# Layer 0's q and k projections as three one-pass products of exact 12-bit parts, with v's projection moved ahead of and between their blocks

## The chip, the cores and the metric

The kernel runs on one core of one Trainium2 chip. A core has TensorE (PE, matrix products, with its weight loads shown apart as PEld), VectorE (DVE), ScalarE (ACT), GpSimd (POOL) and SyncE (SP), which here only issues transfers. The metric is the device time of one execution in microseconds (us); lower is better.

## The reference, cut to what matters

Eight images of 384 channels by 32x32 positions go through two attention layers. The change lies in layer 0 alone:

```python
qkv = (tokens @ qkv_w + qkv_b).reshape(b, n, 3, NUM_HEADS, HEAD_DIM)   # n = 1024, 8 heads of 48
q, k, v = ...
attn = jnp.einsum('bhnd,bhmd->bhnm', q * scale, k) + bias[None]
attn = jax.nn.softmax(attn, axis=-1)
out = jnp.einsum('bhnm,bhmd->bhnd', attn, v)
...
x = x + out @ proj_w + proj_b          # tokens are the group-normalised x
```

All of it is float32. Layer 1 follows: a second attention (6 heads of 64) and a feed-forward part, which takes images 0 to 4 alone.

## The kernel before

The kernel works through layer 0 image by image and then through layer 1 image by image. The order of the instructions on each engine is the order in which the program is written (a manual schedule): each engine takes its instructions in that order, and semaphores alone decide when one may start. SP's order of transfers is the program's order too, so a transfer that waits holds back those behind it.

**Small works by steps.** `later.after(n, work)` puts a piece of work off until `later.step()` has been called n more times; a step is called after each unit of the attention loop and after each block of a projection.

**One image of layer 0.** The image lies in SBUF as `xn`, three tiles of 128 channels by 1024 positions, and is normalised in place. Each q or k projection of a pair of heads is one block (a pair is numbered 0 to 2, `s` is 0 for q and 1 for k, six blocks in all; the fourth pair's channels ride in spare rows of the other three and are copied out by DMA). A block (line 475) is 6 float32 products of 128x128 weights with 128x512 positions, summed over three channel tiles `k` into one PSUM buffer of 128x1024. DVE (line 485, q) or ACT (line 489, k) adds the bias and writes `qk[pair][:, s]`. v's projection (line 503) is four blocks of 6 products of 384 columns, each taken by two DVE adds (line 508).

**The attention loop** runs over 32 units (pair, half of the queries, quarter of the keys). In a unit PE makes the scores of two heads (`s`, line 529), then weighs with the exponentials of the unit two earlier (`o`, line 560; `LAG = 2`). DVE adds the position bias to the scores (line 540, two instructions), and ACT takes the exponential (line 544). Every fourth unit ends an `o`: ACT copies one half (line 568), DVE adds the other (line 571), and after the second half of a pair `divide` sends the sums through DRAM, inverts them on POOL (line 589), spreads them (line 597), multiplies on POOL (line 601), and for the fourth pair issues six copies (line 611). Two units' weighing is left when the loop ends.

**Between two images** the order on PE is: q and k of the next image (six blocks), the two weighings left over, v of the next image (four blocks), the next image's units.

**Buffers.** All PSUM is one pool of four buffers of 128x1024 (`mm2`). Exponentials, and most temporary tiles of 128x1024, come from one pool of nine (`etile`, tag `e`). `qkp` has four q/k tiles. The weights of q, k and v lie in one tile of the tag `w`, of which there is one.

**One-pass products elsewhere.** In layer 1's feed-forward part (lines 1578 and 1629) the operands have the type fp32r, with the activation split into a high and a low part; a matmul on such operands is one instruction record in the trace, while each float32 matmul is two.

## Time and profile before

| | us |
|---|---|
| median of 3 runs | 3038.91 (3038.33 to 3039.49) |
| span of the profiled execution | 3031.8 |
| PE busy in that span | 3010.9 |
| DVE busy | 1777.3 |
| ACT busy | 1401.8 |
| POOL busy | 470.2 |
| one transition between two images of layer 0, image 1 to 2 (364.64 to 415.02) | 50.4 |

The profile is one execution; its span begins with the first instruction and ends with the last, and the measured time lies 7.1 us above it. Busy PE time is the time in which some matmul record is open; records are pipelined and overlap, so that the step from the start of one record to the start of the next, not a record's duration, tells what it costs in a row of many. Rows of groups give line, engine, operation, tiles, shapes and count, then busy us and mean ns of one, then the idle time of the engine before them and what ended it.

### The profile page before, as it was taken

Reading aid. Unit: us, or ns where it says so; the run is one execution under the profiler, and the core shown is the slowest. Engines: PE = TensorE matmul, PEld = TensorE weight load, DVE = VectorE, ACT = ScalarE, POOL = GpSimd, SP = SyncE. Lnnn points to the kernel's source line nnn. Section 1 sums busy time; section 2 is a strip of 40 time slices with the busy share of each in tenths; the row PEclk is TensorE's granted clock in tenths of the full one; section 3 lists DMA queues with packets and bytes.
Section 4 is the critical chain, followed back from the end, with each engine's and each line's share of the span. In section 5 each row is a group of like instructions: output and inputs, shape, how many; then the busy total and the mean of one; then the engine's idle time right before and its main releaser. Section 6 shows DMA issues by size and latency. Waiting matters only on the chain.

```text
span 3031.8 us, 45645 instructions
## 1 busy us (share of the span) xinstructions
PE 3010.9 (99%) x18902; PEld 1622.9 (54%) x18902; DVE 1777.3 (59%) x1765; ACT 1401.8 (46%) x1757; POOL 470.2 (16%) x314
## 2 busy tenths in 40 slices
PE   8999999999999999999999999999999999999999
PEld 3555546455554645555545655655655655645453
DVE  3746637374654727364565765765765755755646
ACT  2633526253452615254463553553653543653534
POOL 2111102121110202102202202202202202211110
PEclk9999999999999999999999999999999999999999
DMA  7512020210202021121401101101101101102011
GB/s 199 146 26 83 19 83 17 72 37 19 83 19 83 23 72 30 26 99 51 116 27 37 50 16 37 50 23 30 50 23 30 50 23 30 50 16 72 16 51 38
DMA packets 102425, 153.47 MB, mean 51 GB/s; under 512 B 59648, under 2 KB 63216, under 8 KB 101184
## 3 DMA queue, kind: packets, MB, share of 16 engines
q1 hardware_dynamic: 98944, 148.63, 17.0%
q8 instruction: 152, 2.49, 0.3%
q10 hardware_dynamic: 3264, 1.82, 0.2%
q14 instruction: 65, 0.53, 0.1%
HBM read 112.29 MB, written 29.07 MB: 47 GB/s over the span
## 4 chain that ended last, share of the span: by engine, by line
PE 93%; DVE 2%; DMA 2%; SPq 1%; ACT 1%; POOL 0%; issue 0%; DVEq 0%; ACTq 0%; POOLq 0%
PE s L529 15%; PE o L560 15%; PE s L1337 11%; PE o L1386 11%; PE pq L475 8%; PE y2p L1629 6%; PE pq L1193 5%; PE pp L624 4%; PE pv L1274 4%; PE y1p L1578 4%; PE pp L1483 4%; PE pv L503 4%; SPq L399 1%; PE sum L1413 1%; PE hs L1222 1%; DVE lun L1530 1%
## 5 line engine op out<-in xcount | busy, mean ns | idle before, releaser
L544 ACT ACTIVATE e<-e 128x1024 f32<-128x1024 f32 x512 | 535.0, 1057 | 441.1 <-DVE e L540 419.9
L540 DVE TENSOR_TENSOR e<-s,grow 128x1024 f32<-128x1024 f32 x512 | 601.1, 1218 | 186.3 <-PE s L529 186.3
L529 PE MATMUL s<-qk 48*64 48x512 f32 x4096 | 607.8, 591 | 2.8 <-DVE e L540 2.7
L560 PE MATMUL o<-e,v 64*64 64x512 f32 x4096 | 603.8, 589 | 0.0
L1348 ACT ACTIVATE e<-s,kc 128x512 f32<-128x512 f32 x768 | 463.9, 694 | 170.6 <-PE s L1337 160.0
L1337 PE MATMUL s<-qk,qk 64*64 64x512 f32 x3072 | 418.3, 592 | 0.2
L1386 PE MATMUL o<-e,v 64*64 64x512 f32 x3072 | 414.8, 590 | 0.0
L529 PEld LDWEIGHTS s<-qk 48*64 48x64 f32 x4096 | 242.2, 132 | 222.1 <-issue 74.9
L560 PEld LDWEIGHTS o<-e,v 64*64 64x64 f32 x4096 | 266.7, 133 | 171.0 <-issue 63.0
L1363 DVE TENSOR_TENSOR t<-t,e 128x1024 f32<-128x1024 f32 x192 | 230.9, 1221 | 53.9 <-ACT e L1348 53.9
L1337 PEld LDWEIGHTS s<-qk,qk 64*64 64x64 f32 x3072 | 153.5, 132 | 189.9 <-issue 110.3
L1193 PE MATMUL pq<-bx,wqkv 128*128 128x512 f32 x576 | 254.1, 596 | 0.7 <-ACT tra L1165 0.7
L475 PE MATMUL pq<-xn,w 128*128 128x512 f32 x576 | 251.8, 598 | 0.0
L1386 PEld LDWEIGHTS o<-e,v 64*64 64x64 f32 x3072 | 157.6, 133 | 171.1 <-issue 143.8
L589 POOL TENSOR_TENSOR inv<-sums,over 128x16 f32<-128x16 f32 x32 | 92.8, 2900 | 956.9 <-DMA sums<-sd 785.4
L475 PEld LDWEIGHTS pq<-xn,w 128*128 128x128 f32 x576 | 109.4, 191 | 142.4 <-issue 139.9
L1193 PEld LDWEIGHTS pq<-bx,wqkv 128*128 128x128 f32 x576 | 107.8, 190 | 143.5 <-issue 139.7
L1360 DVE TENSOR_TENSOR t<-e,e 128x1024 f32<-128x1024 f32 x96 | 114.1, 1224 | 83.0 <-ACT e L1348 83.0
L1565 DVE TENSOR_REDUCE parts<-y 128x1 f32<-128x1024 f32 x75 | 90.1, 1217 | 93.7 <-ACT y L1562 93.2
L1243 POOL TENSOR_TENSOR hc<-hc,rsqrt 128x32 f32<-128x32 f32 x24 | 139.0, 5793 | 2.0
L1209 ACT ACTIVATE qsq<-pq 128x1024 f32<-128x1024 f32 x48 | 49.2, 1025 | 190.1 <-DVE qk L1203 101.9
L485 DVE TENSOR_SCALAR qk<-pq,bqk 128x1024 f32<-128x1024 f32 x24 | 30.8, 1283 | 178.3 <-PE pq L475 178.3
(166 smaller groups left out, 3034.3 us busy)
## 6 DMA issues: line engine op xcount, KB each, us to landing
rb<-rd SPq DMA_DIRECT2D x110, 256.0 KB
xn<-in_x_dram SPq DMA_DIRECT2D x24, 512.0 KB
res<-in_x_dram SPq DMA_DIRECT2D x24, 512.0 KB
x<-res SPq DMA_DIRECT2D x24, 512.0 KB
bx<-x SPq DMA_DIRECT2D x8, 1536.0 KB
rq<-hi SPq DMA_DIRECT2D x48, 256.0 KB
out_dram<-bx SPq DMA_DIRECT2D x23, 512.0 KB
wide<-table SPq DMA_DIRECT2D x80, 114.2 KB
```

Of the source, the lines that this page charges most:

```text
L475: nc.tensor.matmul(pq[:, h], wqk[:, k, s, 2 * pair : 2 * pair + 2, :].rearrange("p h d -> p (h d)"), xn[:, k, ts(h, HALF)], start=(k == 0) ...
L529: nc.tensor.matmul(s[j][ts(c, QP), i], qk[pair][rows, 1, ts(4 * m2 + 2 * i + c, QP)], qk[pair][rows, 0, ts(h, HALF)], start=True, stop=True,)
L540: nc.vector.tensor_add(e.rearrange("p (i q) -> p i q", i=2), s[j], bass.AP(near.tensor, near.offset, [near.ap[0], [-QROWS * IW, 2], [1, HA ...
L544: nc.scalar.activation(e, e, AF.Exp)
L560: nc.tensor.matmul(po[ts(j, S0), r], v[keys, 2 * m2 + i, 2 * pair + j, :], es[j][keys, ts(i, HALF)], start=(m2 == 0 and i == 0), stop=(m2 ...
L1193: nc.tensor.matmul(pq[:, h], wqkv[:, k, s * C + pair * P : s * C + (pair + 1) * P], xt[:, k, ts(h, HALF)], start=(k == 0), stop=(k == KC - 1),
L1243: nc.gpsimd.tensor_tensor(c, c, rsqrt.to_broadcast(list(c.shape)), ALU.pow)
L1337: nc.tensor.matmul(s[j][ts(c, QP), i], qk[pair, 1][rows, ts(4 * m2 + 2 * i + c, QP)], qk[pair, 0][rows, ts(h, HALF)], start=True, stop=True,)
L1348: nc.scalar.activation(e[:, ts(i, HALF)], s[j][:, i], AF.Exp, scale=kc[:, pair, j, m : m + 1])
L1363: nc.vector.tensor_add(total[j], total[j], e)
L1386: nc.tensor.matmul(po[ts(j, D1), r], v[keys, 2 * m2 + i, at : at + D1], es[j][keys, ts(i, HALF)], start=(m2 == 0 and i == 0), stop=(m2 == ...
L1629: nc.tensor.matmul(py[m][:, h], w2[:, k, ts(m, P)], supply.parts[k][i][:, ts(h, HALF)], start=(k == 0 and i == 0), stop=(k == FC - 1 and i ...
```

## The change

q and k of images 1 to 7 are no longer float32 products. The activation and the weights are each cut into parts that hold 12 significant bits: `high` (the low 12 bits of the float's pattern masked off), `low` (the rest), and `high - 4096 low`. A block is then three products of these parts, each over three channel tiles and two halves: high by high and low by 4096 low into one PSUM buffer (`pg`), the two differences into another (`pm`). `pg (1 + 1/4096) - pm / 4096` is the product. So a block has 18 one-pass matmuls in place of 6 float32 ones, two PSUM buffers in place of one, and is taken by ACT (from `pm`, with the bias) and then DVE (from `pg`).

The weights are cut once, during image 0: three pieces of work, put 18, 21 and 24 steps behind, which fall into units 17, 20 and 23. Each has four DVE instructions and one ACT copy on 128x768, takes five `e` tiles and writes three parts to DRAM. From unit 26 of image 0 the tag `w` holds the parts of three blocks at a time; after each of the first three blocks of a transition, that block's place is loaded with the block three further on, and the next transition begins with the three blocks that are there.

The activation is cut per image: three masks on DVE behind units 26, 27 and 28, into q/k tiles that are free then; three ACT copies, three DVE subtractions and three DVE differences at the transition. These nine parts fill the nine `e` tiles.

The order on PE in a transition becomes: first block of v, one weighing, the other weighing, second block of v, three blocks of q/k, third and fourth block of v, three blocks of q/k.

`wv` has a tile of its own, and `bq` holds q's bias times its scale (one small POOL instruction). Image 0's own projections, and layer 1, are as they were.

```diff
-        both = shared.weights("w0")
-        wqk = both[:, 0 : KC * 2 * C].rearrange(
-            "p (k s h d) -> p k s h d", k=KC, s=2, d=S0
-        )
-        wv = both[:, KC * 2 * C :].rearrange("p (k c) -> p k c", k=KC)
+        plain = shared.weights("w0")[:, 0 : KC * 2 * C]
+        wqk = plain.rearrange("p (k s h d) -> p k s h d", k=KC, s=2, d=S0)
+        wv = const.tile([P, KC, C], F32, tag="wv", name="wv")
+        bq = const.tile([P, NF0], F32, tag="bq", name="bq")
...
-        def project_v(b, xn):
-            for m2 in range(MT // 2):
+        blocks = [(pair, s) for pair in range(NF0) for s in range(2)]
+        BB = len(blocks) // 2
+        cut = dram.tile([len(blocks), P, 3, KC, P], F32, tag="cut", name="cut", bufs=1)
+        def masked(out, of):
+            nc.vector.tensor_single_scalar(
+                out.bitcast(INT), of.bitcast(INT), MASK, op=ALU.bitwise_and
+            )
+        def cut_weights(k):
+            w = plain[:, ts(k, 2 * C)]
+            high, low = etile(f"ch{k}")[:, 0 : 2 * C], etile(f"cl{k}")[:, 0 : 2 * C]
+            parts = [etile(f"c{i}_{k}", dtype=F32R)[:, 0 : 2 * C] for i in range(3)]
+            masked(high, w)
+            nc.scalar.copy(parts[0], high)
+            nc.vector.tensor_sub(low, w, high)
+            nc.vector.tensor_scalar_mul(parts[1], low, CUT)
+            nc.vector.scalar_tensor_tensor(parts[2], low, -CUT, high, ALU.mult, ALU.add)
+            for i, part in enumerate(parts):
+                nc.sync.dma_start(
+                    cut[:, :, i, k].rearrange("n p c -> p n c"),
+                    part.bitcast(F32).rearrange("p (n c) -> p n c", c=P),
+                )
+        class Cut:
+            def __init__(self):
+                t = shared.pool.tile([P, KC * 3 * C], F32R, tag="w", name="wc")
+                self.w = t.rearrange("p (n i k c) -> p n i k c", n=BB, i=3, k=KC)
+            def load(self, n):
+                pair, s = blocks[n]
+                nc.sync.dma_start(
+                    self.w[:, n % BB].rearrange("p i k c -> p (i k c)").bitcast(F32),
+                    cut[s * NF0 + pair].rearrange("p i k c -> p (i k c)"),
+                )
+        class Ahead:
...
+            def high(self, k):
+                return self.tile(k // 2)[:, k % 2]
+            def mask(self, k):
+                masked(self.high(k), self.xn[:, k])
+            def highs(self):
+                self.parts = [[], [], []]
+                for k in range(KC):
+                    t = etile(f"xh{self.b}_{k}", dtype=F32R)
+                    nc.scalar.copy(t, self.high(k))
+                    self.parts[0].append(t)
+            def low(self, k):
+                t = etile(f"xl{self.b}_{k}", dtype=F32R)
+                nc.vector.tensor_sub(t, self.xn[:, k], self.high(k))
+                self.parts[1].append(t)
+            def mixed(self, k):
+                t = etile(f"xd{self.b}_{k}", dtype=F32R)
+                nc.vector.scalar_tensor_tensor(
+                    t, self.parts[1][k].bitcast(F32), -CUT, self.high(k), ALU.mult, ALU.add
+                )
+                self.parts[2].append(t)
+            def project(self, weights, n):
+                pair, s = blocks[n]
+                t = self.tile(pair)[:, s]
...
+                ps = mm2("pg" + name), mm2("pm" + name)
+                for i in range(3):
+                    for k in range(KC):
+                        for h in range(NH):
+                            nc.tensor.matmul(
+                                ps[i // 2][:, h], weights.w[:, n % BB, i, k],
+                                self.parts[i][k][:, ts(h, HALF)],
+                                start=(k == 0 and i != 1), stop=(k == KC - 1 and i != 0),
+                            )
+                by = D0**-0.5 if s == 0 else 1.0
+                nc.scalar.activation(
+                    t, flat2(ps[1]), AF.Identity, scale=-by / CUT,
+                    bias=bq[:, pair : pair + 1] if s == 0 else bqk[:, s, pair : pair + 1],
+                )
+                nc.vector.scalar_tensor_tensor(
+                    t, flat2(ps[0]), by * (1.0 + 1.0 / CUT), t, ALU.mult, ALU.add
+                )
+                last = self.tile(NF0)
+                for j in range(2):
+                    nc.sync.dma_start(
+                        last[j * S0 + pair * FR : j * S0 + (pair + 1) * FR, s],
+                        t[j * S0 + D0 : (j + 1) * S0],
+                    )
+                later.step()
+        def project_v(b, xn, some=range(MT // 2)):
+            for m2 in some:
...
+        nc.gpsimd.tensor_scalar(bq, bqk[:, 0], D0**-0.5, 1.0, ALU.mult, ALU.mult)
+        for k in range(KC):
+            later.after(18 + 3 * k, lambda k=k: cut_weights(k))
...
                 later.step()
-            if b + 1 < B:
-                qk = project_qk(b + 1, xn)
-            for done in held:
-                finish = weigh(b, *done)
+                if i == 26 and b == 0:
+                    weights_qk = Cut()
+                    for n in range(BB):
+                        weights_qk.load(n)
+                if b + 1 < B and i >= 26 and i < 26 + KC:
+                    if i == 26:
+                        ahead = Ahead(b + 1, xn)
+                    ahead.mask(i - 26)
+            def weigh_held():
+                finish = weigh(b, *held.pop(0))
                 if finish is not None:
                     finish()
-            if b + 1 < B:
-                project_v(b + 1, xn)
...
+            order = [n % len(blocks) for n in range(b % 2 * BB, b % 2 * BB + len(blocks))]
+            def project(some):
+                for n in some:
+                    ahead.project(weights_qk, n)
+                    if n in order[:BB]:
+                        weights_qk.load((n + BB) % len(blocks))
+            ahead.highs()
+            for k in range(2):
+                ahead.low(k)
+            project_v(b + 1, xn, [0])
+            weigh_held()
+            ahead.low(2)
+            weigh_held()
+            ahead.mixed(0)
+            project_v(b + 1, xn, [1])
+            for k in range(1, KC):
+                ahead.mixed(k)
+            project(order[:BB])
+            project_v(b + 1, xn, [2, 3])
+            project(order[BB:])
+            qk = ahead.qk
```

More of the change, by code (lines that the diff above doesn't have):

```diff
@@ L61 @@
 LAG = 2
+CUT = 4096.0
+MASK = -4096
+INT = mybir.dt.int32
 class _Later:
@@ L205, in _layer0, with etile @@
         rsqrt = shared.rsqrt
-        def etile(name, shape=(P, N)):
-            return ep.tile(list(shape), F32, tag="e", name=name)
+        def etile(name, shape=(P, N), dtype=F32):
+            return ep.tile(list(shape), dtype, tag="e", name=name)
         def flat2(t):
@@ new lines, in _layer0, with __init__, tile @@
+        class Ahead:
+            def __init__(self, b, xn):
+                self.b, self.xn = b, xn
+                self.qk = {}
+            def tile(self, pair):
+                if pair not in self.qk:
+                    self.qk[pair] = qkp.tile([P, 2, N], F32, tag="qk", name=f"qk{self.b}_{pair}")
+                return self.qk[pair]
+            def high(self, k):
[21 more added lines that the diff above has]
+                t = self.tile(pair)[:, s]
+                name = f"{self.b}_{pair}_{s}"
+                ps = mm2("pg" + name), mm2("pm" + name)
[22 more added lines that the diff above has]
+                later.step()
@@ L707, in _layer0 @@
                 later.step()
-            if b + 1 < B:
-                qk = project_qk(b + 1, xn)
-            for done in held:
-                finish = weigh(b, *done)
+                if i == 26 and b == 0:
[8 more added lines that the diff above has]
+                finish = weigh(b, *held.pop(0))
                 if finish is not None:
                     finish()
-            if b + 1 < B:
-                project_v(b + 1, xn)
+            if b + 1 == B:
+                while held:
+                    weigh_held()
+                break
+            order = [n % len(blocks) for n in range(b % 2 * BB, b % 2 * BB + len(blocks))]
[10 more added lines that the diff above has]
+            ahead.low(2)
+            weigh_held()
+            ahead.mixed(0)
[6 more added lines that the diff above has]
+            qk = ahead.qk
         for m in range(KC):
```

## The prediction

> **What bounds the kernel now.** I read the page's totals first, then the chain of waits in order of time around a transition between two images of layer 0, then the timelines of PE and DVE.

> ```profile
> span 3031.8 us, 45645 instructions
> PE 3010.9 (99%) x18902; PEld 1622.9 (54%) x18902; DVE 1777.3 (59%) x1765; ACT 1401.8 (46%) x1757; POOL 470.2 (16%) x314
> PE 93%; DVE 2%; DMA 2%; SPq 1%; ACT 1%; POOL 0%; issue 0%; DVEq 0%; ACTq 0%; POOLq 0%
> ```

> PE is busy throughout and is 93% of the chain that ended last, so what PE no longer does comes off the time, unless a new wait takes its place. The chain at the first transition:

> ```profile
> 188.54 1.72 PE o L560 x15
> 190.26 31.10 PE pq L475 x72
> 221.35 3.60 PE o L560 x32
> 224.95 15.68 PE pv L503 x48
> 240.63 5.85 PE s L529 x45
> ```

> It is all PE: 50.4 us from the first q/k matmul to the first scores (50.37 and 50.38 at the first two transitions). The six blocks take 31.1 us; 72 records at 0.4288 us each would be 30.87, and the remaining 0.2 us is the switch to the next kind. What a one-pass matmul costs is in this trace too, in layer 1's feed-forward part:

> ```profile
> 1641.30 0.62 PE L1578 MATMUL y1p<-lun,w 128*128 128x512 f32 x2
> 1641.75 0.63 PE L1578 MATMUL y1p<-un,w 128*128 128x512 f32 x2
> 1642.22 0.62 PE L1578 MATMUL y1p<-lun,w 128*128 128x512 f32 x2
> 1642.68 0.62 PE L1578 MATMUL y1p<-un,w 128*128 128x512 f32 x2
> ```

> Two matmuls start every 0.463 us, so one costs 0.2316 us (the durations overlap). DVE's prices come from the groups:

> ```profile
> L540 DVE TENSOR_TENSOR e<-s,grow 128x1024 f32<-128x1024 f32 x512 | 601.1, 1218 | 186.3 <-PE s L529 186.3
> L1618 DVE SCALAR_TENSOR_TENSOR ly<-y,hy 128x1024 fp32r<-128x1024 f32 x60 | 74.1, 1235 | 14.9 <-PE y2p L1629 11.3
> L1617 DVE TENSOR_SCALAR hy<-y 128x1024 fp32r<-128x1024 f32 x60 | 41.5, 691 | 10.3 <-ACT y L1609 9.9
> L640 DVE SCALAR_TENSOR_TENSOR res<-pp,bp,res 128x1024 f32<-128x1024 f32 x24 | 30.8, 1284 | 88.8 <-PE pp L624 88.8
> L489 ACT ACTIVATE qk<-pq,bqk 128x1024 f32<-128x1024 f32 x24 | 26.7, 1114 | 210.0 <-PE pq L475 210.0
> ```

> The last view shows what DVE work in the attention loop costs, in image 0:

> ```profile
> 127.63 0.69 DVE L571 TENSOR_TENSOR oT<-o,oT 128x512 f32<-128x512 f32 x1 [1.33 <-ACT oT L568]
> 128.57 0.65 DVE L411 COPY grow<-oT 128x480 f32<-128x480 f32 x1 [0.24 <-DMA oT<-table]
> ...
> 129.14 1.28 DVE L426 BATCH_NORM_STATS2 gst<-xn 128x6 f32<-128x512 f32 x2
> 130.33 2.34 DVE L540 TENSOR_TENSOR e<-s,grow 128x1024 f32<-128x1024 f32 x2
> ...
> 131.59 1.51 PE L529 MATMUL s<-qk 48*64 48x512 f32 x11 [1.81 <-DVE e L540]
> ```

> A unit takes 3.44 us; DVE's two adds take 2.36 and leave a gap of 1.08 us. Here three works stood in one gap, the adds came about 3.0 us late (130.33 in place of about 127.3), and PE lost about 2.5 us (its scores of the unit after next start at 134.67, where 3.44 us a unit gives 132.2). So work of up to 1.08 us behind a unit is free, some 0.55 us more is absorbed, and the rest stops PE.

> [...] a float32 matmul is two records of 0.4288 us[...]; a fp32r one is a single record. [...] the feed-forward shows 231.6 ns, and I take that, keeping 214.4 as the lower end. [...] the trace's two spreads of 256 KB (line 597 issued at 354.00, POOL released at 358.67) took 4.7 us.

> **PE, per transition.** Removed: 72 records x 0.4288 = 30.87 us. Added: 6 blocks x 18 x 0.2316 = 25.01 us. v (48 x 0.3225 = 15.48) and two weighings (3.44) stay. Switches between kinds of matmul cost 0.1 to 0.23 us each (PE's gap before and after line 1222 near 1646.5 is 0.1 and 0.14); there are four before, 0.68 us together, and seven after, about 1.15. Before: 50.47 (50.4 seen). After: 25.01 + 15.48 + 3.44 + 1.15 = 45.08. Gain 5.4 us.

> **What must be ready for the first block.** Let T be the end of the weighing of unit 29. v's first block ends at T + 4.0, the weighings at 5.9 and 7.65, v's second block at 11.7; the first q/k block starts at 11.8 and needs its last `mixed` part 16 matmuls later, at 15.5. DVE in its order: adds of unit 31 until 0.8; two `low`, 1.22 each, until 3.25; v's adds until 5.2; third `low`, which waits for an `e` tile from the first weighing (5.9), until 7.35; line 571, which waits for ACT's copy (8.45), until 9.2; first `mixed` 1.235 until 10.45; v's adds when block two ends, until 12.9; two `mixed` until 15.4. That is just in time: I charge 0.1 us. ACT's three copies (1.05 each, line 1526's price) are over at 5.05, behind the exponentials.

> **Taking the blocks.** ACT 1.11 and DVE 1.28, in series, 2.5 us after a block of 4.17; with four PSUM buffers the next but one is free in time. At the end nothing hides it: DVE is busy with the last block until T' + 2.65 (T' is PE's end), while before, v's last adds were over sooner and line 540 began at 2.2 us after v's end (417.00 against 414.8). DVE sets the pace of the first three units (six adds in a row, 6.88 us), so PE gets this delay: 0.48 us.

> **Weights.** A block's place is loaded (590 KB, about 5 us by the 4.7 above) once PE is done with it, but on SP behind that block's copies, which wait for DVE, and for the third block also behind the six copies of line 611, which wait for POOL and take 4.4 us to issue. With sums out at 9.3, POOL's inverse at 12.4 to 15.3, spread at 19.4, product by 26 and the copies at 27.6 to 32, the third load is issued at 32 and lands at 37.6; its block starts at 40.6. Margin 3 us, cost 0. Without this cover each us late costs 7 us in all.

> **Masks.** One-source, 0.69 us in a gap of 1.08, no line 571 in units 26 to 28: free. No bitwise operation is in the trace; at the two-source price, 1.22, it would be 0.14 over and absorbed.

> So a transition gains 5.4 - 0.1 - 0.48 = 4.8 us, seven of them 33.6 us.

> **Image 0, cutting the weights.** Four DVE instructions on 768 columns: the one-source ones 0.56 each and the two-source ones 0.96 [...], 3.04 and about 3.1 with their waits on each other. Unit 17 also has line 571 and a batch-norm step: the gap is full, 3.3 us late, PE loses 2.8. Units 20 and 23: 3.1 - 1.08 - 0.55 = 1.5 each. The parts hold three `e` tiles until they have landed in DRAM, 393 KB each[...], and those of unit 17 are issued behind `divide`'s wait on POOL (6.8 us after line 571, as 142.82 to 149.63 shows); unit 20's exponentials need these tiles some 10 to 13 us after it. About 1 us more, 0 to 8 at the bounds. Sum 7 us, from 4 to 15. The first three loads have 17 us of units and 11.8 more: hidden.

> **Sum.** 33.6 - 7 = 26.6 us. Span 3031.8 - 26.6 = 3005.2; the runs stand 7.1 us above the span, so the median goes from 3038.9 to 3012.3.

> **Rivals.**
> - *One-pass matmuls reach 214.4 ns*, since a weight is used twice in a row: 756 x 17.2 ns = 13 us more, 2999.3. Against it: the feed-forward uses each four times in a row and shows 231.6. Chance 0.07.
> - *The cut costs more*: the tiles held by DRAM writes, whose 512-byte runs I have no measurement of, bring image 0 to 16 us: 3021.3. For it: SP's queue is blocked just there. Chance 0.10.
> - *Late parts or loads in every transition, moderately*: DVE's chain has no margin at its end, one instruction later is 1.2 us; the third load 1 us past its margin the like. 2 us each, 14 us: 3026.3. Chance 0.11.
> - *Slower: the third load sets the transition.* Place: the sixth block of each transition, PE waiting for a DMA. Price: 7 us for each us beyond the 3 us of margin; with 33.6 - 7 = 26.6 us of gain, slower from 3.8 us of wait on, that is a landing 6.8 us later than worked out. With 6 us of wait, 42 us: 3054.3. For it: SP takes its transfers in order and waits on POOL and DVE ahead of this load. Against it: every step of that chain has its time in the trace. Chance 0.07.

> **How the numbers follow.** My case 0.65, 3012.3; its own range 3006 to 3018 (4.2 to 5.4 us a transition, 5 to 12 us in image 0). The range of 3002 to 3027 takes in the dear cut, the moderate lateness and half of the cheap case. A measurement of this kernel tells 0.2%, 6.1 us, from no change. Faster by more: 0.65 + 0.07 + 0.10 and nearly all of the 0.11, 0.90; within: 0.03; slower 0.07.

> **What would show it.** PE's step in the q/k blocks 0.23 us and a block 4.2; transitions of 45 us; the first line 540 of an image 2.6 us after PE's last block; no PE wait on a DMA in the transitions; PE waits on DVE of 1.5 to 3 us in units 18 to 24 of image 0 alone. Wrong it would be by a step near 0.29 us (18 of them are 5.15 us, the old block), or by waits at the sixth block.

## The result and the profile after

The changed kernel takes 3005.78 us (median of 4 runs, 3004.06 to 3011.10) against 3039.20 us for the kernel before beside it: a ratio of 0.9898, 95% interval 0.9884 to 0.9912. That is 33.4 us less. The profiled execution of after is the run of 3006.06 us.

The head of its page, as for before (busy us, share of the span, instructions):

```profile
span 3004.1 us, 46389 instructions
PE 2974.7 (99%) x19154; PEld 1640.6 (55%) x19154; DVE 1871.5 (62%) x1861; ACT 1447.9 (48%) x1802; POOL 469.4 (16%) x315
```

PE is 36 us less busy than before, and the span is 27.7 us shorter. The difference went into idle time of PE, and most of that lies in image 0, as will be seen. Line numbers of after that recur below: 590 is the q/k block, 596 and 600 its taking by ACT and DVE, 577 the making of a `mixed` part (the difference high - 4096 low), 616 v's projection, 642 the scores and 653 the adds (529 and 540 before), 508 the mask and 520 to 522 the other DVE instructions of the weights' cut, 460 the normalisation and 714 the multiplication on POOL.

First the chain of waits of after in the transition from image 0 to 1 (start us, us, engine, tile, line):

```profile
199.76 4.07 PE pv L616 x12
...
211.49 2.79 PE pg L590 x12
214.28 1.40 PE pm L590 x6
...
243.01 1.42 PE pm L590 x6
244.46 1.12 ACT qk L596
245.60 1.23 DVE qk L600
246.83 2.27 DVE e L653 x2
```

PE has no gap from 199.76 to 244.46: 44.70 us, where before had 50.37. Six matmuls take 1.40 us, that is 0.2333 us each, and a block 4.20. The new thing is the end: ACT and DVE take the last block before DVE can add the bias to the first scores, so the first line 653 begins 2.28 us after PE's last block, where before had 1.93 us (240.63 to 242.56). So a transition gains 5.67 - 0.35 = 5.3 us. The period of an image says the same: 169.14 us after, 174.45 before, 5.31 us for each of seven.

Image 0 pays. This is DVE behind unit 20, in the timeline of after (start us, us, engine, line, operation, tiles, shapes, count, idle time before and who ended it):

```profile
155.70 2.35 DVE L653 TENSOR_TENSOR e<-s,grow 128x1024 f32<-128x1024 f32 x2 [1.08 <-PE s L642]
...
159.65 1.35 DVE L521 TENSOR_SCALAR c<-cl 128x768 fp32r<-128x768 f32 x1
...
161.99 2.35 DVE L653 TENSOR_TENSOR e<-s,grow 128x1024 f32<-128x1024 f32 x2
```

and the timeline of POOL:

```profile
158.91 5.11 POOL L460 TENSOR_SCALAR xn<-xn,gsc 128x1024 f32<-128x1024 f32 x3 [7.31 <-DMA gsc<-back]
```

The adds come 6.29 us after the last ones in place of 3.44. And line 521 took 1.35 us, while the same instruction takes 0.56 behind units 17 and 23; POOL's three instructions beside it took 5.11 us in place of the 3.54 that they take with no cut beside them (first experiment on image 0). PE's three new waits on DVE, in the timeline of PE:

```profile
148.64 2.83 PE L642 MATMUL s<-qk 48*64 48x512 f32 x11 [2.55 <-DVE e L653]
163.27 1.51 PE L642 MATMUL s<-qk 48*64 48x512 f32 x11 [2.46 <-DVE e L653]
175.48 1.51 PE L642 MATMUL s<-qk 48*64 48x512 f32 x11 [1.35 <-DVE e L653]
```

The eleven matmuls after the first wait take 2.83 us, after the others 1.51. The windows view says why (window, its length, busy us of PE, PEld, DVE, ACT and POOL, then the granted PE clock, DMA share and GB/s):

```profile
149.00:151.00 2.00, 2.00 (x12) 0.49 (x8) 0.71 (x1) 1.73 (x2) 1.82 (x3) 0.50 0.03 3
...
152.00:154.00 2.00, 2.00 (x24) 0.72 (x20) 1.74 (x2) 0.48 (x1) 0.00 (x0) 1.00 1.01 284
```

After its stall PE ran at half clock, from 148.6 to 152.0 us: 12 matmuls in 2 us, where it made 24 at full clock from 152 to 154 us.

The difference of the two profiled executions adds up, taken from the starts of the line-653 (before: 540) adds in image 0: from the first of unit 17 to that of unit 31 before has 48.12 us (14 units of 3.44) and after 57.25, 9.13 lost. Units 12 to 17 take 19.97 and 21.50, 1.53 lost, although the cut has not begun: there too PE's clock fell to 0.50, from 131.5 to 134.9 us, after a stall that both kernels have (1.81 us). The first add comes 1.02 us sooner, and units 0 to 12 take 0.14 less. So 7 x 5.31 - 9.13 - 1.53 + 1.02 + 0.14 = 27.7 us, the difference of the spans.

### The profile page after: what moved, and what is told of

It reads as the page before. It is cut to its first block, busy times and chain, and to the rows that moved or that the text cites. A ratio compares the mean times of both kernels' runs of the same rounds, so it can differ in the third digit from the quotient of the medians.

```text
span 3004.1 us, 46389 instructions
## 1 busy us (share of the span) xinstructions
PE 2974.7 (99%) x19154; PEld 1640.6 (55%) x19154; DVE 1871.5 (62%) x1861; ACT 1447.9 (48%) x1802; POOL 469.4 (16%) x315
## 4 chain that ended last, share of the span: by engine, by line
PE 90%; DVE 4%; DMA 3%; SPq 2%; ACT 1%; issue 1%; POOL 1%; DVEq 0%; ACTq 0%; POOLq 0%
PE o L673 14%; PE s L642 14%; PE s L1486 11%; PE o L1535 11%; PE y2p L1778 6%; PE pq L1342 5%; PE pp L737 4%; PE pv L1423 4%; PE y1p L1727 4%; PE pp L1632 4%; PE pg L590 4%; PE pv L616 4%; PE pm L590 2%; SPq L403 1%; DVE e L653 1%; PE sum L1562 1%
## 5 line engine op out<-in xcount | busy, mean ns | idle before, releaser
L1535 PE MATMUL o<-e,v 64*64 64x512 f32 x3072 | 414.8, 590 | 0.0
L642 PEld LDWEIGHTS s<-qk 48*64 48x64 f32 x4096 | 234.9, 132 | 242.5 <-issue 93.7
L673 PEld LDWEIGHTS o<-e,v 64*64 64x64 f32 x4096 | 250.1, 133 | 189.8 <-issue 99.0
L1535 PEld LDWEIGHTS o<-e,v 64*64 64x64 f32 x3072 | 157.6, 133 | 171.1 <-issue 143.8
L1423 PE MATMUL pv<-wqkv,bx 128*128 128x384 f32 x384 | 131.9, 497 | 0.0
L600 DVE SCALAR_TENSOR_TENSOR qk<-pg,qk 128x1024 f32<-128x1024 f32 x42 | 51.4, 1225 | 128.2 <-ACT qk L596 128.2
L1423 PEld LDWEIGHTS pv<-wqkv,bx 128*128 128x128 f32 x384 | 119.1, 315 | 19.0 <-issue 9.7
```

Source lines behind the costliest of these rows:

```text
L642: nc.tensor.matmul(s[j][ts(c, QP), i], qk[pair][rows, 1, ts(4 * m2 + 2 * i + c, QP)], qk[pair][rows, 0, ts(h, HALF)], start=True, stop=True,)
L673: nc.tensor.matmul(po[ts(j, S0), r], v[keys, 2 * m2 + i, 2 * pair + j, :], es[j][keys, ts(i, HALF)], start=(m2 == 0 and i == 0), stop=(m2 ...
L1423: nc.tensor.matmul(pv[:, i, 0:C], xt[:, k].rearrange("c (p m) -> c m p", m=MT)[:, 2 * m2 + i], wqkv[:, k, 2 * C : 3 * C], start=(k == 0), ...
L1535: nc.tensor.matmul(po[ts(j, D1), r], v[keys, 2 * m2 + i, at : at + D1], es[j][keys, ts(i, HALF)], start=(m2 == 0 and i == 0), stop=(m2 == ...
```

## The experiments

All times are medians, each beside runs of the kernel before, whose medians lay between 3036.55 and 3038.76 us. Line numbers in the experiments' traces are those of their own text; where they differ the operation is named.

### What the transition gains, and from what

**The order alone.** Kernel before, float32 blocks, with all of v moved ahead of them (not quite the change's order, which has two of v's blocks between the q/k blocks):

```diff
             if b + 1 < B:
-                qk = project_qk(b + 1, xn)
+                project_v(b + 1, xn, [0])
             for done in held:
                 ...
             if b + 1 < B:
-                project_v(b + 1, xn)
+                project_v(b + 1, xn, [1, 2, 3])
+                qk = project_qk(b + 1, xn)
```

> The kernel before, with float32 q/k blocks, in a new order of the transition: v's first block, the two weighings, v's other three blocks, then the six q/k blocks. Theory (the gain lies in the products, the order only hides the parts' making): PE has the same work, 50.4 us a transition; the units start behind a q/k block and its eviction rather than behind v, up to 0.5 us later each: 3039 to 3043, ratio 1.000 to 1.0015. Rival (v's new place itself gains, as it fills a wait between the loop and the blocks): 1 us a transition or more, 3032 or less, which would be a fifth of what the change gains there.

Measured 3035.86 us, ratio 0.9999 (0.9991 to 1.0008). The chain of its transition between images 1 and 2:

```profile
364.83 4.07 PE pv L503 x12
...
415.20 4.98 PE s L529 x35
```

50.37 us, as before, and the period is 174.45 us as well. This order gains nothing by itself. The loss at the restart that I had allowed for did not come either; here one engine alone takes each block, which would explain it. The gain is the products'.

**The step of a matmul.** The same 18 matmuls with the halves outermost, so that the weights change at each:

```diff
+                for h in range(NH):
                     for i in range(3):
                         for k in range(KC):
-                            for h in range(NH):
```

> The 18 matmuls of a block in another order: all nine of one half of the positions, then all nine of the other, so that the weights change at every matmul and not at every second. Theory (the step of 0.232 us is that of a one-pass fp32r matmul and doesn't depend on the use of a weight twice in a row): step 0.231 to 0.235 us, block 4.2 us, the last halves of the mixed parts are wanted no later, time 3006 within 2 us. Rival (a repeated weight saves something, or a change of weights costs 15 ns or more): 756 matmuls by 17 ns, 13 us more or beyond, 3019.

Measured 3025.33 us, ratio 0.9952 (0.9940 to 0.9964), 20 us slower than the change. By the time alone the rival would have won. The timeline of PE in the first block of a transition says otherwise:

```profile
221.67 0.50 PE L590 MATMUL pm<-xd,wc 128*128 128x512 f32 x1 [0.62 <-DVE xd L577]
222.81 0.50 PE L590 MATMUL pm<-xd,wc 128*128 128x512 f32 x1 [0.64 <-DVE xd L577]
223.15 0.86 PE L590 MATMUL pg<-xh,wc 128*128 128x512 f32 x3
```

From the third row on, three matmuls start every 0.70 us (223.15, 223.85, 224.55 and so on): 0.2333 us each, just as in the change. A weight used twice saves nothing here. What costs is that the third `mixed` part is wanted eight matmuls (1.9 us) sooner, and PE waits for DVE. I had written that the parts were wanted no later, and that was wrong: the period is 170.93 us, 1.79 more than the change's, seven times 12.5 us. So the change's order has next to no slack on DVE: of 1.9 us sooner, 1.79 were paid. The profiled execution is the slowest of six. Of the other 7 us or so in it, 5 lie in image 0's units and 3 ahead of its first add, where the instructions are the same as in the change (below).

**Parts and loads without v's cover.**

```diff
-            project_v(b + 1, xn, [0])
             weigh_held()
             ...
-            project_v(b + 1, xn, [1])
             ...
             project(order[:BB])
-            project_v(b + 1, xn, [2, 3])
             project(order[BB:])
+            project_v(b + 1, xn)
```

> The three-product blocks with v behind them: both weighings, six q/k blocks in a row, then v's four blocks. Theory (v ahead and between is there to hide the parts and, above all, the third weight load): the first block starts 8 us sooner than its parts allow, 1 to 2 us lost on DVE; the sixth block would start at T + 26 (T the end of unit 29's weighing), while the third load is still issued at T + 32 behind the six copies of line 724 and lands at T + 37.6, so PE waits on a DMA about 11 us; 12 to 14 us a transition in all, 84 to 98 us in the kernel: 3090 to 3104, much slower than before. Rival (the load isn't tied to the copies, or lands sooner): only the parts, 1 to 2 us a transition, 3013 to 3020. Rival (the order doesn't matter): 3006.

Measured 3047.49 us, ratio 1.0036 (1.0023 to 1.0049): slower than before, and 42 us slower than the change, where I had expected 84 to 98. The periods are 173.8 to 176.5 us, some 5.7 more than the change's. The waits of PE in the transition from image 1 to 2 (waiter, who ended it, us in all, times, longest):

```profile
PE pg L590 <- DMA wc<-cut: 3.0, 1, 3.0
PE pm L590 <- DVE xd L577: 1.0, 3, 0.4
```

Most of the rest is the clock: after the 3.0 us, PE ran at 0.50 for 3.4 us. My expectation was too large because the six copies of line 724 are put off by steps, and with two v blocks fewer ahead of them they fall behind the third load, which was issued first here (396.45, the copies at 400.66). So it is loads in general, and the parts, that v covers; the tie of the third load to the copies is not tested by this run. The wait of 3.0 us, in the timeline of PE:

```profile
392.58 1.56 PE L590 MATMUL pg<-xh,wc 128*128 128x512 f32 x6
...
399.98 2.90 PE L590 MATMUL pg<-xh,wc 128*128 128x512 f32 x6 [3.04 <-DMA wc<-cut]
```

The blocks begin at 378.04, 384.18, 388.38, 392.58 and 399.98 us, so it is the fifth that waits. Its parts come with the second load, issued at 393.45 behind the two spreads of line 710 (392.18). The trace's packets of 4.6 KB, which only these loads have, end at 391.8 us for the first load, 398.8 for the second and 401.2 for the third, and the semaphore that releases PE is complete at 399.84.

**The margin of the third load.** Six, and then twelve, more transfers on SP behind the copies of line 724:

```diff
+                    for more in range(6):      # 12 in the second
+                        row = SP + (more % NF0) * FR
+                        nc.sync.dma_start(extra[more % (2 * NF0)], oT[row : row + FR, pair])
```

> The changed kernel with six more transfers of the same size (16 rows of 4 KB, to a DRAM tile that nobody reads) behind the six copies of line 724, so that the third weight load of a transition is issued 3.7 us later, at T + 35.6. Theory (in the trace the transfers of the third load end 3.4 us after its issue, 5 us ahead of its block): no wait of PE on a DMA, time as the changed kernel within 2 us, 3006 to 3008. Rival (it lands 5 us after issue or later, as the margin of 3 us in the prediction took it): PE waits 0.3 to 1 us, 2 to 7 us more over seven transitions, 3009 to 3014.

> The same with twelve more transfers: the third load is issued about 7.4 us later, at T + 39.3, while its block would start at T + 40.3. Theory (landing 3.4 us after issue): PE waits for a DMA 2.4 us before the sixth block of each transition, 17 us in seven, and a few more if the PE clock falls after it: 3022 to 3032. Rival (landing 5 us after issue): 4 us each, 28 us and more: 3034 or above, about as slow as before. Rival (the block doesn't wait for this load): 3007.

With six: 3011.28 us, ratio 0.9914 (0.9901 to 0.9928). The load was issued 3 us later (2.89 us of transfers), PE waits for no DMA in any of the seven transitions, and the period is 169.14 us, the change's own. The median is 3 us above what I had put down, but it isn't the load: image 0 took 122.78 us in this profile and 119.05 in the change's.

With twelve: 3030.29 us, ratio 0.9972 (0.9962 to 0.9983), as the theory had it. Two of its transitions, in the timeline of PE:

```profile
423.62 1.63 PE L590 MATMUL pg<-xh,wc 128*128 128x512 f32 x6 [1.35 <-DMA wc<-cut]
...
596.24 2.71 PE L590 MATMUL pg<-xh,wc 128*128 128x512 f32 x6 [3.23 <-DMA wc<-cut]
```

and the window behind the second wait (columns as above):

```profile
597.00:599.00 2.00, 2.00 (x6) 1.57 (x5) 0.00 (x0) 0.00 (x0) 0.00 (x0) 0.50 0.23 39
```

The sixth block waits for its load, and a wait of 3.23 us brings half clock with it (6 matmuls in 2 us), one of 1.35 doesn't; of two in between, 1.83 us brought it and 1.85 didn't. The seven waits are 14.1 us in all, where I had put down 17. The period rises by 1.6 us in some images and 5 in others, 3.1 on average. The profiled execution is the slowest of eight: image 0 also lost 10.5 us against the change's profile. The slower case of the prediction is thus real, with its place and its price; it begins somewhere between the 2.9 us more of SP's time that were free and the 7.2 us of the twelve transfers.

### What image 0 costs

**No cut.** The four DVE instructions and the ACT copy left out, plain weights sent to DRAM in place of the parts:

```diff
-            high, low = etile(...), etile(...)
-            parts = [etile(...) for i in range(3)]
-            masked(high, w)
-            nc.scalar.copy(parts[0], high)
-            ...
+            parts = [w] * 3
```

> The four DVE instructions and the ACT copy of the weights' cut are left out; the plain weights go to DRAM three times in place of the three parts, so q and k of images 1 to 7 are computed from other weights, with the same matmuls, transfers and evictions. Theory (the cut costs image 0 its DVE work in the gaps behind units 17, 20 and 23): the pairs of line 653 stay 3.44 us apart there, except about 1.4 us at unit 17 and nothing at 20 and 23; PE's three stalls go; the first transition starts 7.5 to 9 us sooner, the time falls by 8 to 9 us against the changed kernel, to about 2997.5, ratio to before 0.986. Rival (most of image 0's loss has another cause, as the PE clock or the earlier start): less than 4 us, 3002 or more. The transitions stay at 44.7 us and the period of an image at 169.1 us in both.

Measured 2998.98 us, ratio 0.9877 (0.9863 to 0.9891): 6.4 us less than the change by the two ratios, and 9.5 by the two profiled executions, of which this one is the fastest of its four; I had expected 8 to 9. The fourteen units of image 0 from 17 on take 48.11 us, 3.44 each, as before (unit 17 itself 3.68 and the next 3.19, in both), and PE has a single wait on DVE from 100 us to the end of image 0, the old one:

```profile
131.32 1.51 PE L636 MATMUL s<-qk 48*64 48x512 f32 x11 [1.81 <-DVE e L647]
```

So the transitions are worth 7 x 5.31 = 37 us, which is this kernel's gain, and cutting the weights takes 6 to 9 us of it.

**The change again**, beside the next ones:

> The changed kernel itself, unaltered, beside the next ones, to see how far its runs lie apart. Theory (its runs differ through image 0: how long DVE stops PE, whether the cut of unit 20 meets POOL, and whether the PE clock falls after it): 3003 to 3012, ratio to before 0.9895; the period of 169.1 us is the same to 0.1 us whatever the time; the interval from the first pair of scores to the last pair of image 0 takes up the differences. Rival (the spread lies in layer 1 or in the transitions): image 0's interval is the same as before, 120.2 us.

3008.08 us (3005.77 to 3009.32), ratio 0.9901 (0.9887 to 0.9915). Six of the executions here have the same instructions in image 0 up to its transition. From their traces, the time in us from the first add of a unit to that of another:

```
                      units 0-12   12-17   17-31
before                   40.44     19.97   48.12
no cut                   40.44     19.74   48.11
the change               40.30     21.50   57.25
the change again         40.50     22.42   57.22
halves outermost         40.45     19.80   63.84
v behind                 40.95     20.67   56.75
six more transfers       41.98     23.66   57.14
twelve more              41.70     23.84   64.03
```

The period of the later images is 169.1 to 169.2 us in both executions of the change; image 0 isn't one number. Between these two profiles, 2.6 us apart, it makes 1.1 us, and 1.4 lie behind the first add of the last image, almost all of that in layer 1: my expectation held for less than half of the difference. The column of units 12 to 17 follows the clock after the old stall near 130 us: 19.7 to 20.7 where no half clock follows it, 21.5 and 22.4 where it lasts 3.4 us, 23.7 and 23.8 where it lasts 6.8. In units 17 to 31 the cut costs 9 us in four executions and 16 in two. In those two, this is what stands behind unit 20. The timeline of DVE in the kernel with the halves outermost:

```profile
162.28 1.83 DVE L520 TENSOR_TENSOR cl<-w,ch 128x768 f32<-128x768 f32 x1
164.25 2.48 DVE L521 TENSOR_SCALAR c<-cl 128x768 fp32r<-128x768 f32 x1
```

the timeline of POOL:

```profile
159.46 3.85 POOL L460 TENSOR_SCALAR xn<-xn,gsc 128x1024 f32<-128x1024 f32 x3 [6.59 <-DMA gsc<-back]
```

and the timeline of PE:

```profile
169.01 2.83 PE L642 MATMUL s<-qk 48*64 48x512 f32 x11 [5.32 <-DVE e L653]
```

POOL's two works (line 714 follows line 460) begin 1.4 us ahead of the cut and not 0.9 us behind its start, and three of the four DVE instructions take 1.9 to 4.4 times their length (the mask 1.39 us in place of 0.55, and the two shown); the fourth, alone again, takes its 0.94. PE waits 5.32 us, and its eleven matmuls at 2.83 us are at half clock again (0.50 from 167 to 173 us in the windows). What makes an instruction of DVE wait beside POOL is not shown; the traces show which ones do. Line 521 ends 0.4 us behind the end of POOL's line 714 (166.73 and 166.31), as if nearly all of it had waited for that. Line 653, with one operand in PSUM, keeps its 1.22 us beside POOL: in the change the two from 161.99 us on take 2.35 together, while POOL's line 460 lasts until 164.02. Line 522 keeps its length there as well (0.94 us from 160.92 on). The runs of halves outermost have two groups, 3016.65 and 3017.89, and 3024.96 to 3026.14; the profiled one is of the second.

**The cut elsewhere.** Behind units 16, 19 and 24:

```diff
-            later.after(18 + 3 * k, lambda k=k: cut_weights(k))
+            later.after((17, 20, 25)[k], lambda k=k: cut_weights(k))
```

> The same three pieces of cutting with the same instructions, behind units 16, 19 and 24 in place of 17, 20 and 23: away from line 684 and the batch-norm step of unit 17, and from POOL's works of units 21 to 23. Theory (beyond the 3.0 us of DVE, what costs is what stands in the same gap and POOL beside it): each piece 3.1 - 1.08 - 0.55 = 1.4 us, 4.3 us in image 0, all four DVE instructions at 0.55 to 0.96 us, PE's stalls below 1.6 us, no fall of the PE clock: 2.5 to 4 us sooner than the changed kernel, about 3002.5. Rival (the place doesn't matter, a piece costs 2.5 us anywhere): 3006.

3007.50 us, ratio 0.9902 (0.9888 to 0.9916): no gain. The DVE instructions now take 0.55 to 0.96 us everywhere, PE's waits are 1.42 to 2.15, and the clock stays up after them. But a new wait stands behind unit 20:

```profile
161.04 2.36 DVE L653 TENSOR_TENSOR e<-s,grow 128x1024 f32<-128x1024 f32 x2 [3.46 <-DMA cut<-c]
```

The adds wait for an `e` tile that a transfer of parts to DRAM still holds. Units 17 to 31 take 54.25 us, 3 less than the change, but 12 to 17 hold one piece as well, and take 23.49 (with 3.4 us of half clock after the old stall, as in the change's 21.50). The time is near the rival's 3006, for another reason than the rival's.

**The cut on POOL**, all but mask and copy:

```diff
-            nc.vector.tensor_sub(low, w, high)
-            nc.vector.tensor_scalar_mul(parts[1], low, CUT)
-            nc.vector.scalar_tensor_tensor(parts[2], low, -CUT, high, ALU.mult, ALU.add)
+            nc.gpsimd.tensor_sub(low, w, high)
+            nc.gpsimd.tensor_scalar(parts[1], low, CUT, 1.0, ALU.mult, ALU.mult)
+            nc.gpsimd.tensor_sub(parts[2], high, parts[1].bitcast(F32))
```

> The mask stays on DVE (0.55 us a piece) and the copy on ACT, the low part, its multiple and the difference go to POOL (about 1.8, 0.95 and 1.8 us, by the price of line 714 for 1024 columns), so the five e tiles of a piece are held some 4 us longer. Theory (DVE's time in the gap is what costs): PE's waits of 1.4 to 2.5 us in units 18, 21 and 24 fall below 0.7 us, image 0 is 7 to 8.5 us shorter, the time about 2998 (2996 to 3000). Rival (e tiles held until they lie in DRAM cost image 0 its time): the pairs of line 653 in units 19 to 26 wait for e tiles, no gain or a loss, 3005 or more. Second rival (POOL beside DVE slows DVE): masks take over 1 us in place of 0.55, gain 4 to 6 us, 3000 to 3002.

3014.08 us, ratio 0.9924 (0.9911 to 0.9937), 8 us slower than the change. DVE's longest waits from 143 to 190 us (in all, times, longest):

```profile
DVE e L653 <- POOL c L521: 10.8, 3, 4.5
```

The first rival in kind: tiles are short, although POOL's instructions and not the transfers hold them here. The count of tiles would explain it: the exponentials have six of the nine tiles (three units in flight, two each), so a piece may hold three beyond its own gap; no run here varies that count alone. The masks keep their 0.55 us, but POOL does nothing beside any of the three, so that the second rival is not tested here.

**Smaller pieces.** Six pieces of 384 columns, three tiles each, then nine of 256 with one lasting tile each, the multiple on ACT in both; last the nine with their transfers issued by ACT:

```diff
-        for k in range(KC):
-            later.after(18 + 3 * k, lambda k=k: cut_weights(k))
+        for j, at in enumerate((15, 16, 18, 19, 20, 21, 24, 25, 26)):      # six: 15, 16, 18, 19, 20, 24
+            later.after(at + 1, lambda j=j: cut_weights(j // 3, j % 3))
...
-            for n in range(2): nc.sync.dma_start(cut[2 * two + n, :, :, k], ...)
+            for n in range(2): nc.scalar.dma_start(cut[2 * two + n, :, :, k], ...)      # the last one alone
```

> The cut in six pieces of 384 columns behind units 15, 16, 18, 19, 20 and 24, the multiple by 4096 on ACT; three DVE instructions a piece (0.36 + 0.56 + 0.56 us, worked out from the 768-column ones), three e tiles in place of five. Theory (up to 1.6 us of DVE behind a unit is free): pieces cost 0 to 0.4 us each, the row 18 to 20 together about 0.6, image 0 within 1.5 us of the kernel with no cut at all: about 3000 (2998.5 to 3001.5), the ratio to before 0.987 to 0.988. Rival (tiles held until they lie in DRAM, with more pieces in the air): pairs of line 653 wait for e tiles, 3003 or more.

> The cut in nine pieces of 256 columns, behind units 15, 16, 18, 19, 20, 21, 24, 25 and 26 (the masks of the activation behind 27, 28 and 30); the multiple by 4096 on ACT, three DVE instructions of 0.3 to 0.42 us a piece, one e tile for high and low (free at once) and one for the three parts. Theory (two limits together: at most 1.6 us of DVE behind a unit, and at most three e tiles held by transfers to DRAM, as six of the nine are in use): no wait of line 653 on a DMA, PE's waits on DVE below 0.5 us but for unit 21 and 25, where line 684 stands too (0.3 each), image 0 from the first pair to the last pair of scores 109 to 111 us against 120 in the changed kernel and 108.3 with no cut: 3000 to 3002, ratio to before 0.987 to 0.9885. Rival (the tiles are still held too long, as SP waits for POOL at unit 18): one or two waits of 2 us and more on a DMA, 3004 or more.

> The nine pieces again, with their transfers to DRAM issued by ACT in place of SP, where they stood behind a transfer that waits for POOL (unit 17's divide and the batch-norm statistics, until 157.6 us). Theory (SP's order held the e tiles, not the transfers' own length): the 4.2 us wait of line 508 on a DMA at unit 20 goes, PE's longest wait on DVE in units 15 to 27 is below 1.5 us, the first pair to the last pair of image 0 takes 110 to 113 us: 3001 to 3004, ratio to before 0.987 to 0.989. Rival (the transfers themselves, in pieces of 512 bytes, are what holds the tiles): the wait stays above 2 us, 3008 or more. Rival (issuing on ACT delays the exponentials by 1 to 2 us a piece): PE waits on ACT in the units after 15 to 21, no gain, 3008 or more.

Measured 3010.26 us (0.9909, 0.9894 to 0.9923), 3011.05 us (0.9914, 0.9901 to 0.9928) and 3007.69 us (0.9900, 0.9884 to 0.9917). All three expectations failed: none is faster than the change. DVE's own work was as cheap as worked out (0.35 + 0.56 + 0.56 us in the halves, 0.28 + 0.42 + 0.43 in the ninths away from POOL's line 460 and multiplication), and in the ninths the units with the pieces behind 16, 18 and 19 stay 3.3 to 3.5 us apart: those pieces are free. Then DVE waits (in the halves already behind unit 16, 1.95 us for a transfer). The halves, in the view of waits:

```profile
DVE e L655 <- DMA cut<-c: 5.2, 1, 5.2
```

the ninths, in the timeline of DVE:

```profile
161.74 0.73 DVE L508 TENSOR_SCALAR ch<-w 128x256 int32<-128x256 int32 x1 [4.21 <-DMA cut<-c]
```

and the timeline of SP in the ninths has the reason: the parts of units 18 and 19, ready at 152 to 155 us, stand behind transfers that wait for POOL:

```profile
154.13 0.34 SPq L705 DMA_DIRECT2D rd<-inv  x1
...
157.63 3.55 SPq L526 DMA_DIRECT2D cut<-c  x4
```

Issued by ACT (third kernel) they leave at 148 to 152 us, and that 4.21 us wait is gone; in its place comes one of 2.27 us on a transfer, a piece behind unit 21 that meets POOL (1.22 us for the mask, 2.45 for the subtraction, in place of 0.28 and 0.43), and half clock after a PE stall of 2.96. So the transfers' own time, the first rival there, seems to count too: the wait is above its 2 us, and the time just below its 3008. Four limits stand close together here: DVE's gap, the tiles, SP's order, and what DVE loses beside POOL (a subtraction of 0.43 us took 2.45). None of the versions tried beats the change; about 2999 us is what one with a free cut would reach.

## Why the prediction was right

- **The number.** 3005.78 us lies within 3002 to 3027, but just below the 3006 to 3018 that I gave my own case, and 6.5 us below its 3012.3. Of these, 5.1 are the way from span to time (last point), 1.1 the span, and 0.3 the profiled run's place above the median. That the span came so close is in part luck: the transitions gained 3.6 us more than worked out (7 x 5.31 against 33.6), and image 0 cost 2.5 us more (9.5 against 7).
- **Step and block.** 0.2316 us a matmul was taken from layer 1, 0.2333 measured; block 4.2. The rival's 214.4 ns was my estimate, half of the 428.8 ns of one record of a float32 matmul, and is out: using a weight twice or once makes no difference.
- **The transition.** 4.8 us predicted, 5.31 measured. Three small terms were too dear: with the blocks as measured the switches between kinds come to 44.70 - 25.20 - 15.48 - 3.44 = 0.58 us and not 1.15, the `mixed` parts cost nothing, the restart 0.35 and not 0.48. (The 2.2 us that I read in before are 2.0: v ends at 415.0 us and not at 414.8.) The blocks, 0.19 dearer, and a transition of 50.37 and not 50.47 before take 0.3 back. "Just in time" was meant literally and was so: the run with the halves outermost paid 1.79 us for 1.9 us less of time.
- **Third load.** Issued at T + 31.9 as worked out, and no wait. Its margin was under-sized: DMA traffic ends at 235.0, 3.4 us after the issue and 5 ahead of the block, where I had landing in 5 to 6 us and a margin of 3. PE was released 4.6 us after the issue where it did wait (591.61 in the timeline of SP, 596.24), so some of the 5 us seems to go to the signal (1.0 us in the run with v behind, from the last packet of the second load at 398.8 to the semaphore at 399.84). 2.9 us more on SP were free, 7.2 were not, as the two runs with more transfers show.
- **Masks.** 0.68 us each, units 26 to 28 stay 3.44 us apart: free, as said.
- **Image 0.** 7 us predicted, 9.1 in the profile, 6.4 by the ratios. The pieces: unit 17 2.8 predicted and 4.55 seen, of which 1.4 is half clock, which the prediction had nowhere; unit 20 1.5 and 2.67, of which 0.8 is line 521 beside POOL, also nowhere; unit 23 1.5 and 1.89, so the 0.55 us that PE was to absorb was nearer 0.15. The 0.56 and 0.96 us for the instructions on 768 columns were an estimate; unit 17 shows 0.55, 0.96, 0.56 and 0.95. The 1 us for tiles held by transfers didn't come in this kernel, perhaps since three-unit steps leave the transfers time (the packets of unit 17's three parts end at 155.68, 5.2 us after the first of them was issued at 150.49); the other placements show it is there, at 2.3 to 5.2 us. The dear-cut rival named the right mechanism for kernels other than this one; and its price of 16 us did come in two executions with this kernel's image 0, through POOL beside the cut and the clock.
- **From span to time.** The span was put at 3005.2 us and is 3004.1. The time was put at 3012.3 and is 3005.78: 7.1 us were added because before's runs stood so far above its profile. After's profiled run stands 1.96 us above its span, so most of the 7.1 was not a constant distance, but a profiled execution quicker than the three timed ones. Every run on record with a span of its own lies 1.7 to 2.1 us above it. By 1.96, before's 3031.8 is a run of 3033.8, and such runs of before are there among the later ones (3033.52 to 3042.34). The forecast of the difference, 26.6 us, was nearer to that of two profiles (27.7) than to that of two medians (33.4).

## What to carry to other kernels

When a change buys one cheap steady state with a one-time preparation, price the preparation by every resource that it shares and not by its instructions: the gap of the engine, the tiles that it keeps, the queue that must free them, and the engine that works beside it (line 521 took 1.35 us in place of 0.56 beside POOL). A gap that is a quarter empty on one of these can be full on the next, so that moving or splitting the work only changes which one binds. A stall that the preparation causes may cost half clock as well, by where it falls and not by its length alone (3.41 us of it behind a stall of 2.55 us here, none behind one of 2.46). And single executions with the same instructions in image 0 differ there by up to 11 us here (118.4 and 129.6 from its first add to that of its last unit): look apart at the stage that is the same in all of them and at the stage that isn't.

## What the hardware did that I had not expected

```profile
128.09:131.50 3.41, 1.60 (x13) 0.52 (x16) 3.41 (x5) 1.55 (x3) 1.70 (x1) 1.00 0.08 16
131.50:134.91 3.41, 3.41 (x20) 1.07 (x16) 3.13 (x4) 1.76 (x2) 0.67 (x1) 0.50 0.08 5
145.16:148.57 3.41, 0.93 (x9) 0.04 (x1) 3.38 (x6) 0.62 (x1) 1.45 (x1) 1.00 0.02 2
148.57:151.98 3.41, 3.34 (x16) 1.04 (x20) 1.14 (x2) 2.11 (x2) 2.70 (x5) 0.50 0.19 50
158.81:162.22 3.41, 2.00 (x20) 0.42 (x12) 3.14 (x4) 1.64 (x3) 3.31 (x2) 1.00 0.76 203
162.22:165.63 3.41, 2.36 (x23) 1.29 (x27) 3.10 (x4) 2.12 (x2) 3.41 (x3) 1.00 0.84 239
```

The stall of 1.81 us left PE busy for 1.60 us of one window, that of 2.55 us for 0.93, and the next window is at half clock. The stall of 2.46 us is divided between two windows, with 2.00 and 2.36 us busy, and the clock stays. In before the 1.81 us are divided too (2.45 and 2.56). Over the windows of all traces from 35 us on, by PE's records, whose ends are modelled: after 1.95 us of idling or more the next window was at half clock in 27 of 27, after 1.43 to 1.90 in 13 of 29, and after less (windows at half clock themselves left aside) twice in some 12,100, both near 80 us (in before 0.95 us of idling, then 0.50 from 82.95 us on). So the idling inside one window goes with the clock closely but not strictly, and what sets the clock is not shown beyond that. Against the kernel's start the windows lie differently from one execution to the next: the first stretch at 0.50 begins at 82.95 us in before, 14.2 windows ahead of the change's at 131.50. This can be a good part of the chance in image 0.

- **DVE beside POOL.** A one-source instruction of 0.55 us took 1.2 to 2.5, a two-source one of 0.96 took 1.83, and POOL's own three took 5.11 us in place of 3.54.
- **The step of a fp32r matmul** of 128x512 is 0.2333 us with new weights each time as with a weight used twice.
